# Five edits to a metaformer and mixture-of-experts kernel: where the time step's rows are spread, how the C rows, the gate and the depthwise taps are issued, and which engine adds the last image's softmax sums

## The chip, the cores and the metric

The kernel runs on one core of a Trainium2 chip. The metric is the device time of one launch in microseconds (us), as the median of several runs. Engines are named as in the profile: PE is TensorE, DVE is VectorE, ACT is ScalarE, POOL is GpSimd, and SP is SyncE, whose queue issues most DMA transfers.

## The reference, cut to what matters

The input is four images of 256 channels by 32 x 32 positions (N = 1024 positions, all in fp32). For each image the reference computes, in this order:

```python
xc = layernorm(x).reshape(B, N, 4, 64)          # four groups n of 64 channels
# for each group a Mamba block: 128 inner channels d, 16 states s
u, z = split(xc_n @ inw_n.T); u = silu(conv4(u))
dt = softplus((u @ xpw_n.T)[:, :4] @ dtw_n.T + dtb_n); Bm, Cm = the next 16 and 16 columns
h[d, s] = exp(dt * A[d, s]) * h[d, s] + dt * u * Bm[s]      # scan over the 1024 positions
y = sum_s h[d, s] * Cm[s] + u * D
xm_n = (y * silu(z)) @ outw_n.T + skip * xc_n
# convolutions, with 3-tap depthwise ones
g = sigmoid(conv1x1(depthwise3_grouped(xm)));  xg = g * xm
R = conv1x1(depthwise3(xg)) + xg
xm2 = conv1x1(depthwise3(concat[xs, R])) + xs
# beside each other: a depthwise convolution, and attention with 8 heads of 32
x_out = gelu(layernorm(concat[depthwise3(xm2), mha(xm2)] @ fc))
x_out = proj(layernorm(depthwise3x3(instance_norm(x_out))))
# then, for all 4096 positions: layer norm, a router (8 experts, top 2), two-layer experts with gelu
```

## The kernel before, in words

**Order of the work.** All engines run in the order in which Python emits instructions (a manual schedule), so the program's order is the queue of each engine. Two things make that order. The scan loop emits one *step* after the other; generators (the other stages) are advanced by `beat()`, which is called once behind each step, a *tick*. A generator that yields k is resumed k ticks later.

**The scan.** There are 32 *parts* (b, n, h): image b, channel group n (`NB` = 4), half h of the positions (512 each). A part has 16 steps i = 4q + g: g picks 32 of the 128 inner channels, q four of the 16 states, so one step is 128 rows (32 channels x 4 states) by 512 positions. In a step, `decay` (L653, ACT) makes dA = exp(dt A) three steps ahead, `inflow` (L663, DVE) makes dBu into a PSUM bank one step ahead, `step` runs the DVE scan instruction (L674) and then a POOL product with the spread C rows (L682). `spread_b` (L645) and `sums_of` (L687, L692) are PE matmuls, once per q. All PSUM tiles come from one pool of eight banks, all 128 x 512 temporaries from a pool of 16 (`act2`).

**What is emitted at which step for the next part.** The dictionaries `before`, `behind` and `group` say it. For the next part: `project_dt` at step 0, `softplus` at 2, `sum_dt` at 4 and `times_u` at 5 (both POOL), and `spread_dt` at 10, 11, 13 and 14: four DMAs each on SP's queue, copying 32 rows of dt and dt u to each of the four state groups. `spread_c` (four DMAs per q) is emitted at steps 0, 4, 8 and 13. In the second half of a group, `project_c` and `copy_c` for the next group stand at steps 3 and 5 (its first half) and 7 and 9 (its second half): a matmul of 16 rows into a bank, an ACT copy of 16 x 512, and a DMA to DRAM. For the part just finished, `project_out` stands at step 6 and `add_skip` at 8.

**Beside the scan.** When the scan of image b begins, the generator `convolutions(b - 1)` starts. It runs beside the parts (b,0,0), (b,0,1), (b,1,0) and (b,1,1), which are 64 ticks. Behind the last step of (b,1,1) a `drain()` advances the generators until the convolutions are done; then `attention(b - 1)` runs, with the scan stopped until its last blocks. The last image's convolutions and attention come behind the whole scan. There, expert tiles (`tiles`, L1994 and L2004) fill PE between the convolutions' pieces; for the attention they are held back.

**The convolutions.** In order: load (4 ticks); `depthwise3` on the input `xl`, per channel half c: the first tap on ACT (L424), then two taps on DVE (L429); the grouped convolution `qd` on PE; `gate`/`sigmoid` (L860, L870): two banks for each c, then two sigmoids that read PSUM, with a load of the sigmoid table in front and of the log/exp table behind; the product with `xm` on POOL (L878); `depthwise3` on `xm`; four products `rp` with their residual copies on ACT (L889); `depthwise3` on the result (`d4r`); four products `fp`, two ticks apart (L918); four products `vp`; eight products `qkp` (L998).

`in_turn` is what makes pipelines of a product and its use:

```python
        def in_turn(items, make, use, lag=2, every=1):
            made, lag = [], lag // every
            for at in range(len(items) + lag):
                if at >= lag:
                    use(items[at - lag], made[at - lag])
                if at < len(items):
                    made.append(make(items[at]))
                yield every
```

**Attention.** A block is (g, h): four heads and half of the queries; there are four blocks per image, each of `NK` = 8 steps kt over keys. A step: four logit matmuls `st` (L1023), four ACT exponentials `e` (L1033), four matmuls with the values (`av`, L1069). Of each pair of steps the exponentials are added on DVE (L1079, four adds), and four matmuls with ones (L1043) add the pair's sums into a second bank. At a block's end: Ln and Exp on ACT (L1051, L1056), a maximum (L1055) and a product (L1059) on DVE. The generator `local` puts six depthwise taps (L440, L445) on DVE beside the attention.

Of the kernel before, what the change touches and what calls it, by code (L numbers as in the profile page):

```python
# [9 lines left out]
F32 = mybir.dt.float32  # L10
# [62 lines left out]
def network(  # L73
# [70 lines left out]
    with tc.tile_pool(name="w_conv", bufs=1) as wp, tc.tile_pool(  # L144
# [277 lines left out]
        def depthwise3(dst, c, src, c_src, w, wi, bias):  # L422

            nc.scalar.activation(  # L424
                dst[:, c, :], src[:, c_src, 0:N], AF.Identity, bias=bias, scale=col(w, 3 * wi)
            )
            yield 1
            for k in (1, 2):
                nc.vector.scalar_tensor_tensor(  # L429
                    dst[:, c, :], src[:, c_src, k : k + N], col(w, 3 * wi + k), dst[:, c, :],  # L430
                    ALU.mult, ALU.add,
                )
                yield 1

# [188 lines left out]
        def project_c(b, n, h):  # L623
            cp = T[b, n, h, "cp"] = ps(f"cp_{b}_{n}_{h}")
            nc.tensor.matmul(
                cp[0:DS], xpwT_s[:, n, DTR + DS :], T[b, n, "u"][:, half(h)], start=True, stop=True
            )

        def copy_c(b, n, h):
            c_rows = a2(f"c_{b}_{n}_{h}", DS)  # L630
            nc.scalar.copy(c_rows, T[b, n, h, "cp"][0:DS])
            cd = T[b, n, h, "cd"] = spread.tile([DS, HALF], F32, tag="cd", name=f"cd_{b}_{n}_{h}")
            nc.sync.dma_start(cd, c_rows)
# [77 lines left out]
        def add_skip(b, n, h):  # L711
# [7 lines left out]
            1: [(sums_of, GS - 1)], 3: [(gather,)], 6: [(project_out,)], 8: [(add_skip,)],  # L719
# [4 lines left out]
            10: [(spread_dt, 0)], 11: [(spread_dt, 1)],  # L724
# [8 lines left out]
            {3: [(project_c, 0)], 5: [(copy_c, 0)], 7: [(project_c, 1)], 9: [(copy_c, 1)]},  # L733
# [3 lines left out]
        def first_part():  # L737
# [18 lines left out]
            for h in range(2):  # L756
                project_c(0, 0, h)
                copy_c(0, 0, h)
# [68 lines left out]
        def convolutions(b):  # L827
# [6 lines left out]
            for c in range(NC2):  # L834
                yield from depthwise3(d[0], c, xl, c, "fdw_w", c, col("fdw_b", c))
# [19 lines left out]
            def gate(c):  # L855
                gp = []
                for h in range(2):
                    gp.append(ps(f"gp_{b}_{c}_{h}"))
                    r = ts(h, 64)
                    nc.tensor.matmul(  # L860
                        gp[h], qpwT_s[r, ts(c, P)], qs[r], start=True, stop=True
                    )
                return gp

            gs = []

            def sigmoid(c, gp):
                gs.append(a4(f"g_{b}_{c}"))
                for h in range(2):
                    nc.scalar.activation(  # L870
                        gs[c][:, half(h)], gp[h], AF.Sigmoid, bias=col("qpw_b", c)
                    )
                loaded[0] = None
                log_exp()

            yield from in_turn(range(NC2), gate, sigmoid)
# [5 lines left out]
            for c in range(NC2):  # L882
                yield from depthwise3(d[1], c, xm, c, "rdw_w", c, col("rdw_b", c))
# [23 lines left out]
            for c in range(NC2):  # L907
                for ticks in depthwise3(
                    d[1], c, xm, c, "fdw_w", NC2 + c, col("fdw_b", NC2 + c)
                ):  # L910
                    next(gated, None)
                    yield ticks
# [91 lines left out]
        def attention(b):  # L1004
# [30 lines left out]

            log_exp()
            ahead = logits(*steps[0])
            pairs, accs, ending = [], [None, None], []

            def sum_pair():  # L1040
                kt, acc, es = pairs.pop()
# [19 lines left out]
            for at, (g, h, kt) in enumerate(steps):  # L1061
# [11 lines left out]
                if pairs:  # L1073
                    sum_pair()
# [1078 lines left out]
```

## Time and profile before

| | us |
|---|---|
| median of 3 runs (2289.41 to 2292.67) | 2289.62 |
| the profiled execution's own time | 2288.33 |
| its span in the trace | 2286.6 |
| PE busy | 2030.7 |
| DVE busy | 1556.7 |
| ACT busy | 1222.6 |
| POOL busy | 1066.4 |
| mean granted clock of PE | 0.937 of full |

Busy times are sums over the whole span. The stages have different limits, so the prediction reads the span stretch by stretch. Times of a stretch are counted from the span's start. In rows of groups, the columns are: line, engine, operation, output<-input tiles, shapes, count | busy us, mean ns of one | idle us just before them and what ended it. In a row of a table of stretches each engine has its busy us and, in brackets, its instructions.

### The profile page before, as it was taken

To read this page: it belongs to the slowest core of one execution; us is meant where nothing else is said; L and a number is where in the kernel's file an instruction comes from. 1 tells how busy PE (TensorE), PEld (TensorE's weight loads), DVE (VectorE), ACT (ScalarE), POOL (GpSimd) and SP (SyncE) were. 2 spreads that over 40 slices of the span, in tenths; PEclk is the share of its full clock that TensorE was granted. 3 is DMA by queue.
4 is the path that set the end of the run, shared out by engine and by line. 5 is a ranking of instruction groups with operands and counts; after the bars stand their busy time and mean duration, and the time that the engine had idled before them with its cause. 6 is when DMAs were issued, how large, how long until landed. Compare 5 with 4: busy or idle time off the path is not lost. (4 is left out here: it accounts for less than half of the span.)

```text
span 2286.6 us, 28565 instructions
## 1 busy us (share of the span) xinstructions
PE 2030.7 (89%) x8858; PEld 908.8 (40%) x8858; DVE 1556.7 (68%) x2217; ACT 1222.6 (53%) x2297; POOL 1066.4 (47%) x929
## 2 busy tenths in 40 slices
PE   6878878999977999986799999679999999999995
PEld 2112112332212322322123223125743768888884
DVE  3989998767899878799887877986254353211111
ACT  4665666677767666664666767334267422222221
POOL 0788878613688630675985035554040123322221
PEclk8887999999998999996899999679999999999997
DMA  3554453301453321333433013343230266877765
GB/s 98 139 155 123 125 135 89 99 10 51 98 139 86 92 48 38 93 89 95 133 89 99 19 34 78 84 157 110 87 108 1 63 198 202 243 195 195 195 175 159
DMA packets 160846, 252.86 MB, mean 111 GB/s; under 512 B 35300, under 2 KB 105348, under 8 KB 160680
## 3 DMA queue, kind: packets, MB, share of 16 engines
q1 hardware_dynamic: 140800, 225.46, 35.6%
q0 software_dynamic: 13264, 17.85, 4.1%
q10 hardware_dynamic: 6616, 7.58, 1.0%
q8 instruction: 74, 1.21, 0.2%
q14 instruction: 92, 0.75, 0.1%
HBM read 141.31 MB, written 33.98 MB: 77 GB/s over the span
## 5 line engine op out<-in xcount | busy, mean ns | idle before, releaser
L682 POOL TENSOR_TENSOR dA<-hs,cs 128x512 f32<-128x512 f32 x512 | 683.2, 1341 | 459.1 <-DVE hs L674 303.2
L653 ACT ACTIVATE dA<-dts,A 128x512 f32<-128x512 f32 x512 | 358.9, 717 | 169.7 <-DMA dts<-dt 82.2
L692 PE MATMUL yp<-dA,quads 128*32 128x512 f32 x1024 | 297.6, 667 | 86.3 <-POOL dA L682 61.8
L2020 POOL DMA_INDIRECT Y<-ys,dest x70 | 114.5, 1635 | 524.8 <-DVE ys L2014 518.5
L1033 ACT ACTIVATE e<-st 128x512 f32<-128x512 f32 x512 | 263.9, 603 | 97.4 <-PE st L1023 90.3
L663 DVE TENSOR_TENSOR dBu<-dts,bs 128x512 f32<-128x512 f32 x384 | 261.0, 680 | 76.2 <-PE bs L645 24.5
L1999 ACT ACTIVATE hs<-h,b 128x256 f32<-128x256 f32 x280 | 116.6, 472 | 354.5 <-PE h L1994 206.5
L2004 PE MATMUL y<-w,hs 128*128 128x256 f32 x1120 | 256.0, 380 | 2.8 <-ACT hs L1999 2.8
L1994 PE MATMUL h<-xT,w 128*128 128x256 f32 x1120 | 251.8, 381 | 5.1 <-DVE xT L1972 5.1
L674 DVE TENSOR_TENSOR_SCAN hs<-dA,last,dBu 128x512 f32<-128x512 f32 x192 | 244.2, 1272 | 5.0 <-ACT sq_lgn L1115 1.3
L674 DVE TENSOR_TENSOR_SCAN hs<-dA,dBu 128x512 f32<-128x512 f32 x192 | 232.3, 1210 | 9.9 <-issue 4.4
L1994 PEld LDWEIGHTS h<-xT,w 128*128 128x128 f32 x1120 | 212.9, 191 | 42.4 <-issue 7.8
L1079 DVE TENSOR_TENSOR e<-e,e 128x512 f32<-128x512 f32 x256 | 169.1, 723 | 86.2 <-ACT e L1033 51.8
L1972 DVE COPY xT<-xp 128x512 f32<-128x512 f32 x35 | 24.2, 691 | 295.7 <-PE xp L1971 295.7
L2004 PEld LDWEIGHTS y<-w,hs 128*128 128x128 f32 x1120 | 209.6, 190 | 38.4 <-issue 8.7
L645 PE MATMUL bs<-u,xpwT_s 128*32 128x512 f32 x1024 | 170.2, 678 | 53.1 <-DVE hs L674 27.4
L1023 PE MATMUL st<-qk 32*128 32x512 f32 x1024 | 173.0, 638 | 1.6 <-DVE hs L674 1.6
L692 PEld LDWEIGHTS yp<-dA,quads 128*32 128x32 f32 x1024 | 51.6, 115 | 307.2 <-POOL dA L682 177.9
L1069 PE MATMUL av<-e,v 128*32 128x512 f32 x1024 | 139.5, 604 | 0.0
L1023 PEld LDWEIGHTS st<-qk 32*128 32x128 f32 x1024 | 59.3, 183 | 115.3 <-issue 86.2
L1043 PE MATMUL av<-e,every 128*32 128x512 f32 x512 | 86.7, 594 | 4.1 <-DVE e L1079 4.1
L663 DVE TENSOR_TENSOR bs<-dts,bs 128x512 f32<-128x512 f32 x128 | 86.6, 676 | 2.2 <-DMA dts<-dt 2.2
(295 smaller groups left out, 2725.3 us busy)
## 6 DMA issues: line engine op xcount, KB each, us to landing
w<-in_W_dram SPq DMA_DIRECT2D x136, 512.0 KB, 4.5
dts<-dt SPq DMA_DIRECT2D x512, 128.0 KB, 2.3
cs<-cd SPq DMA_DIRECT2D x512, 64.0 KB, 2.1
xs<-XS SPq DMA_DIRECT2D x35, 260.0 KB, 4.5
xd<-xn SPq DMA_DIRECT2D x64, 128.0 KB, 2.5
b<-in_b_dram SPq DMA_DIRECT2D x35, 128.0 KB, 4.8
xn<-in_x_dram SPq DMA_DIRECT2D x8, 512.0 KB
XL<-xl SPq DMA_DIRECT2D x8, 512.0 KB, 2.7
```

The costliest lines, as they stand in the source:

```text
L645: nc.tensor.matmul(bs[r], xpwT_s[:, n, s : s + 1].to_broadcast([P, 32]), T[b, n, "u"][:, half(h)], start=True, stop=True,)
L653: nc.scalar.activation(dA, T[b, n, h, "dts", g][:, 0, :], AF.Exp, scale=A[:, g, n, q : q + 1])
L663: nc.vector.tensor_tensor(dBu, T[b, n, h, "dts", g][:, 1, :], T[b, n, h, "bs", q], ALU.mult)
L674: nc.vector.tensor_tensor_scan(hs, T[b, n, h, "dA", i], dBu, 0.0 if h == 0 else last, ALU.mult, ALU.add)
L682: nc.gpsimd.tensor_tensor(dA, hs, T[b, n, h, "cs", q], ALU.mult)
L692: nc.tensor.matmul(T[b, n, h, "yp"][ts(g, 32)], quads, T[b, n, h, "dA", q * GD + g], start=False, stop=(q == GS - 1),)
L1023: nc.tensor.matmul(sts[i], k[r, ts(kt, P)], q[r, half(h)], start=True, stop=not shifted)
L1033: nc.scalar.activation(es[i], sts[i], AF.Exp, scale=1.0 / HD**0.5)
L1069: nc.tensor.matmul(accs[0][ts(i, HD)], v8[:, kt, ts(4 * g + i, HD)], es[i], start=(kt == 0), stop=(kt == NK - 1),)
L1079: nc.vector.tensor_tensor(first[i], first[i], es[i], ALU.add)
L1994: nc.tensor.matmul(hp[:, i, :], w1(c, k), xT[:, c, :], start=(c == 0), stop=(c == NC2 - 1))
L2004: nc.tensor.matmul(yp[:, ts(t, C)], hs[:, k, ts(t, P)], w2(k), start=(k == 0), stop=(k == NHC - 1))
```

## The change

1. `spread_dt` for g = 0 and 1 stands at steps 7 and 9 instead of 10 and 11. `project_out` stands at step 7 (6 before), `add_skip` at 9 (8 before).
2. `project_c` makes both halves at step 3, as 32 rows each (B and C rows) in one bank; `copy_c` at step 6 copies 64 rows once, and two DMAs store the two halves' 16 C rows.
3. `depthwise3` takes both channel halves: the two first taps on ACT, one tick apart, then one more tick, then the four DVE taps.
4. The gate makes one bank per tick; ACT copies each with its bias (Identity), and behind the four copies two sigmoids of 1024 columns run from SBUF.
5. Attention: `total`, the bank of the sums, is taken with the first sum; a block's Ln and Exp stand directly behind the last sum, and its two DVE instructions in front of the next step's adds. For the last image the group of steps whose exponentials are added on DVE is all eight (`group = NK`), and the matmuls with ones run once per block.

```diff
-        def depthwise3(dst, c, src, c_src, w, wi, bias):
...
+        def depthwise3(dst, src, w, wi, bias):
+            for c in range(NC2):
+                nc.scalar.activation(
+                    dst[:, c, :], src[:, c, 0:N], AF.Identity, bias=col(bias, wi + c),
+                    scale=col(w, 3 * (wi + c)),
+                )
+                yield 1
+            yield 1
+            for c in range(NC2):
+                for k in (1, 2):
+                    nc.vector.scalar_tensor_tensor(
+                        dst[:, c, :], src[:, c, k : k + N], col(w, 3 * (wi + c) + k), dst[:, c, :],
+                        ALU.mult, ALU.add,
+                    )
+                    yield 1
...
+        def project_c(b, n):
+            cp = T[b, n, "cp"] = ps(f"cp_{b}_{n}")
+            for h in range(2):
+                nc.tensor.matmul(
+                    cp[ts(h, 2 * DS)], xpwT_s[:, n, DTR:], T[b, n, "u"][:, half(h)],
+                    start=True, stop=True,
+                )
+        def copy_c(b, n):
+            c_rows = a2(f"c_{b}_{n}", 4 * DS)
+            nc.scalar.copy(c_rows, T[b, n, "cp"][0 : 4 * DS])
+            for h in range(2):
...
+                nc.sync.dma_start(cd, c_rows[ds(2 * DS * h + DS, DS), :])
...
-            1: [(sums_of, GS - 1)], 3: [(gather,)], 6: [(project_out,)], 8: [(add_skip,)],
+            1: [(sums_of, GS - 1)], 3: [(gather,)], 7: [(project_out,)], 9: [(add_skip,)],
...
-            10: [(spread_dt, 0)], 11: [(spread_dt, 1)],
+            7: [(spread_dt, 0)], 9: [(spread_dt, 1)],
...
-            {3: [(project_c, 0)], 5: [(copy_c, 0)], 7: [(project_c, 1)], 9: [(copy_c, 1)]},
+            {3: [(project_c,)], 6: [(copy_c,)]},
...
+            yield from in_turn(
+                CO_H, gate, lambda at, gp: nc.scalar.activation(
+                    gs[at[0]][:, half(at[1])], gp, AF.Identity, bias=col("qpw_b", at[0])
+                ),
+            )
+            for c in range(NC2):
+                nc.scalar.activation(gs[c], gs[c], AF.Sigmoid)
+            loaded[0] = None
+            log_exp()
+            yield 1
...
+            group = NK if b == B - 1 else 2
+            ready, total, ending = [], None, None
+            def invert(g, h, values, total):
+                low = a2(f"low_{b}_{g}_{h}")
+                nc.scalar.activation(low, total, AF.Ln, bias=added)
...
+            def end_block(g, h, values, total, low):
+                at = (2 * b + g) * 2 + h
+                if not shifted:
+                    nc.vector.tensor_reduce(sums[:, 0, at : at + 1], total, AX.X, ALU.max)
+                nc.vector.tensor_tensor(OT[b][g][:, half(h)], values, low, ALU.mult)
+            def sum_group():
...
+                return invert(g, h, values, total) if kt == NK - 1 else None
...
+                if ending:
+                    end_block(*ending)
+                ending = sum_group() if ready else None
+                if kt % group == 0:
                     first = es
                 else:
                     for i in range(4):
                         nc.vector.tensor_tensor(first[i], first[i], es[i], ALU.add)
-                    pairs.append((kt, accs[1], first))
-                    if ending:
-                        end_block(*ending.pop())
-                if kt == NK - 1:
-                    ending.append((g, h, *accs))
+                if kt % group == group - 1:
+                    ready.append((g, h, kt, values, first))
```

## The prediction

> **What bounds the kernel now.** I read the page first, then a table of stretches, then groups and the timeline inside the stretches that the edits touch.
>
> ```profile
> span 2286.6 us, 28565 instructions
> PE 2030.7 (89%) x8858; PEld 908.8 (40%) x8858; DVE 1556.7 (68%) x2217; ACT 1222.6 (53%) x2297; POOL 1066.4 (47%) x929
> ```
>
> PE's 89% is an average. Parts of the scan with nothing beside them last 27.3 to 28.3 us (16 scan starts 1.7 to 1.8 apart) and DVE never waits there; the rest is mixed. The table takes image 2: parts (2,0,0), (2,0,1), (2,1,0), (2,1,1) up to the first logit matmul, the attention beside the stopped scan, and last the attention of the last image.
>
> ```profile
> core 0: us, PE busy (x) PEld busy (x) DVE busy (x) ACT busy (x) POOL busy (x), PEclk, DMA share, GB/s
> 676.60:711.20 34.60, 25.50 (x103) 6.50 (x102) 33.30 (x37) 26.52 (x49) 27.96 (x22) 0.95 0.54 139
> 711.20:751.60 40.40, 32.23 (x116) 8.63 (x114) 36.80 (x39) 28.14 (x41) 33.74 (x24) 0.87 0.36 89
> 751.60:791.20 39.60, 38.33 (x124) 14.33 (x125) 30.52 (x36) 21.68 (x45) 25.64 (x20) 1.00 0.36 89
> 791.20:821.80 30.60, 30.40 (x121) 11.28 (x119) 27.84 (x31) 21.00 (x38) 23.44 (x20) 1.00 0.39 92
> 821.80:918.70 96.90, 95.91 (x638) 26.51 (x634) 77.36 (x106) 70.39 (x140) 6.07 (x5) 1.00 0.09 24
> 1677.80:1764.20 86.40, 86.40 (x642) 24.52 (x641) 51.41 (x79) 69.52 (x137) 19.96 (x27) 1.00 0.13 39
> ```
>
> In the first two rows DVE is the bound and PE idles 9.1 and 8.2 us; from the third row to the end of the attention PE has almost no gap (1.3, 0.2, 1.0). In the last row PE is busy all the time. From 1600 us to 2235 PE idles only some 10 us in all, so the tail is PE work laid end to end.
>
> What DVE waits for in part (2,0,1), and in part (2,1,0):
>
> ```profile
> L429 DVE SCALAR_TENSOR_TENSOR d<-xm,V,d 128x1024 f32<-128x1024 f32 x4 | 6.1, 1528 | 3.6 <-ACT d L424 3.6
> ```
>
> ```profile
> L663 DVE TENSOR_TENSOR dBu<-dts,bs 128x512 f32<-128x512 f32 x13 | 8.9, 683 | 7.2 <-ACT u L582 3.2 <-ACT xm L715 3.1 <-PE bs L645 0.6
> ```
>
> The 3.6 is ACT being late with the first tap. The 7.2 is different: ACT itself waits there for PE (6.5 us for `up`, 5.0 for `op`), whose queue is full of `fp` products.
>
> Last image's attention, from the timeline: two steps, and the end of the last block.
>
> ```profile
> 1691.61 2.50 DVE L1079 TENSOR_TENSOR e<-e,e 128x512 f32<-128x512 f32 x4 [0.43 <-PE av L1069]
> 1692.31 1.14 PE L1023 MATMUL st<-qk 32*128 32x512 f32 x8
> 1693.38 1.07 PE L1069 MATMUL av<-e,v 128*32 128x512 f32 x8
> 1693.47 4.13 ACT L1033 ACTIVATE e<-st 128x512 f32<-128x512 f32 x8 [1.07 <-PE st L1023]
> 1694.03 2.48 DVE L445 SCALAR_TENSOR_TENSOR xloc<-xl,V,xloc 128x1024 f32<-128x1024 f32 x2
> 1696.54 1.04 PE L1043 MATMUL av<-e,every 128*32 128x512 f32 x8
> 1697.51 0.71 PE L1023 MATMUL st<-qk 32*128 32x512 f32 x4
> ```
>
> ```profile
> 1760.67 2.50 DVE L1079 TENSOR_TENSOR e<-e,e 128x512 f32<-128x512 f32 x4 [2.70 <-ACT e L1033]
> 1762.13 2.14 PE L1043 MATMUL av<-e,every 128*32 128x512 f32 x8
> 1764.30 0.69 ACT L1051 ACTIVATE low<-av,added 128x512 f32<-128x512 f32 x1 [2.83 <-PE av L1043]
> 1765.02 0.69 DVE L1055 TENSOR_REDUCE sums<-av 128x1 f32<-128x512 f32 x1 [1.86 <-ACT low L1051]
> 1765.78 0.69 DVE L1059 TENSOR_TENSOR qk<-av,low 128x512 f32<-128x512 f32 x1
> ```
>
> A pair of steps takes 5.20 us (1692.31 to 1697.51), all PE. ACT needs 4.13 of them, DVE 2.50 for four adds.
>
> **The change, part by part.**
>
> *Last image's sums.* Per block, four sets of `ones` matmuls (1.0 us each) become one: 12 us of PE go, in four blocks. Adds go from 4 to 7 sets of 2.50. Then PE needs 8 x 2.07 + 1.0 = 17.6 us per block, ACT 8 x 2.07 + 1.5 = 18.0, DVE 17.5 for adds. But a block's end is now serial: the last add ends at 1763.17, the product at 1766.47, so 3.3 us pass through PE, Ln and the maximum, and the next block's adds stand behind the product. DVE's period is 17.5 + 3.3 = 20.8 us against 21.3 now (second logit sets of successive blocks start at 1704.85, 1726.14, 1747.43). The six `local` taps (1.6 + 2.5 + 2.5 us), which lie in DVE's idle time now, are no longer hidden. First adds 3.75 us behind the first logits, as now; 4 x 17.5 + 3 x 3.3 + 6.6 = 86.5 more; last add at 90.2 us where it is at 85.4: **+4.8**. Bounds: -2 (taps hidden, four blocks 0.5 shorter each) to +9 (PE, now 85% busy, falls to half clock for some 3 us per block, as it does in the stretches of 0.95 and 0.87 above). PE work saved gives nothing, because the tiles are held until the attention is over. The Trainium skill, "PSUM — Partial Sum Buffer", PSUM bank collisions raise a hardware error, has two engines on one bank kept apart by semaphores; the row that shows DVE's maximum waiting for ACT's Ln agrees, and it speaks against this edit.
>
> *Length of the convolutions.* Counting yields: before, 4 + 6 + 3 + 1 + 4 + 2 + 6 + 4 + 6 + 12 + 6 + 10 = 64 ticks (load, taps, `qd`, its copy, gate, product, taps, `rp`, taps, `fp`, `vp`, `qkp`), exactly the four parts. After: each `depthwise3` has 7, the gate 7, so 70. Everything behind the gate comes 4 to 6 ticks later, and six ticks fall into the drain.
>
> *(b,0,0).* First taps in front and single gate banks remove DVE's waits for ACT's `d` and `g`: 2.5 us for image 1, 1.2 for image 2, 6.0 for image 3: **-9.7** in all.
>
> *(b,0,1).* The 3.6 goes (DVE's first tap is three ticks behind ACT's, not one) and two of the `d4r` taps (1.25 each) move on: -6.1. Against it, the sigmoids now come in a lump at step 4: loads 2 x 1.28 and 2 x 1.05 (row of the equally wide `z` silu), 4.7 us, behind softplus (2.7), four copies (2.8), y (0.6) and five decays (3.6): 14.4 us of ACT in steps that last 8.9; decays run three steps (5.3 us) ahead. Bounds 0 and 3.7 of new DVE wait; I take 1.5, near the lower end because ACT is ahead otherwise. POOL's `xm` products now follow dt in its queue and end before DVE's taps. **-4.6** x 3 = -13.8. Loads go from four to two per image, 2.6 us of ACT; copies cost 2.7 and sigmoids 2.1 where four took 2.7: nothing. By the Trainium skill, "ScalarE: Activation LUTs", What ACT_TABLE_LOAD costs, a switch also pays a drain of about 1.38 us, which would save another 2.8; here a sigmoid starts 0.02 us behind its 1.28 load, so I leave that out.
>
> *(b,1,0) and (b,1,1).* In the new program's order the last two `rp` products fall behind the boundary: half of 7.5 + 4.2 us, +5.9 of PE. The `fp` products stand behind steps 9, 11, 13, 15 instead of 3, 5, 7, 9. Until step 9 DVE then sets the pace: 9 x 1.71 + 4 x 1.25 = 20.4 us. PE has there what it has now up to 769.5 less two `fp` products (16.6 - 9.9), plus 5.9, about 14 with the leftovers: 6.4 us idle, 5.1 more than the 1.3 now. From there PE is full until the first logits (in the drain three `qkp` products). Cost 5.9 + 5.1 = 11; if PE starts `fp` one step early (its sums are ready then), 9. I take **+9** x 3 = 27. Bounds: 0 (all of it hides in DVE's time) and 14 (the drain's six ticks at DVE-step length, 10.5, instead of 5.2).
>
> *dt rows earlier.* ACT waits 82.2 us for them in 29 waits, but DVE does not wait for ACT there: pure parts run at 27.3 with these waits in them. What moves: eight DMAs per part pass in front of `spread_c` at step 8, on SP's queue. SP's longest wait for dt u is 5.2 us, and those C rows are used at step 12, four steps (6.8 us) on. **0**, bounds -3 and +3.
>
> *C rows in one bank.* 16 ACT copies of 0.57 us go (9.1), two DMAs come together at step 6; matmuls stay. ACT is not the bound where they stand: 0, bounds -3 and 0. `project_out` and `add_skip` one step later: their wait (3.1) is PE's queue, so 0.
>
> *Attention of images 0 to 2* keeps pairs, PE stays full, Ln comes one step earlier: 0 +- 2. *Last image's convolutions* are six ticks longer, but tiles fill PE meanwhile and the attention still starts behind the fifth tile: 0, bounds -2 and +3.
>
> Sum: 4.8 - 9.7 - 13.8 + 27 = +8.3 on the profiled execution's 2288.3, 2296.6; the median of the runs is 1.3 higher. I say **2297**.
>
> **Rivals.**
>
> *Faster (0.25).* The shifted products hide: PE work is the same in total, and if the spread of `fp` over (b,1,0) and (b,1,1) leaves no new gap, the +27 is near 0 and the waits removed are gained. For it: DVE has 8.1 us of waits in (2,1,0) that a different order could dissolve. Against: PE has no gap left there to hide 5.9 us in. 4.8 - 9.7 - 13.8 = -18.7: 2271. It decides for faster as soon as the +9 is under +2 per image.
>
> *No change (0.15).* The +9 is about 5 to 7, or the attention's +4.8 is 0: 2285 to 2294.
>
> *Much slower (0.08).* The drain is exposed in full (14 instead of 9 per image: +15) and the last attention pays 9: 2288.3 + 8.3 + 15 + 4.2 = 2316.
>
> *My forecast (0.52)*: 2294 to 2312.
>
> **How the numbers follow.** 0.2%, about what a measurement of this kernel can tell from no change, is 4.6 us. Faster has the first rival's 0.25 less its edge, 0.24; same 0.16; slower 0.60. The range leaves out the lower half of the first rival and most of the third: 2277 to 2314. The likeliest case's own range is 2294 to 2312.
>
> **What would show it.** In the profile after: no wait of L429 for ACT in (b,0,1), and that part near 36 us; PE gaps of 4 us or more in the first half of (b,1,0); image 2's way from its first scan step to its first logits 2 to 4 us longer than 145.2; four blocks of the last attention 20 to 21 us apart, DVE busy nearly throughout, PE with gaps at each block's end, and the whole near 91 us. I am wrong if PE is without gaps in (b,1,0), if the drain costs nothing, or if the last attention gets shorter than 86.

## The result, and the profile after

The changed kernel takes 2330.89 us (median of 4 runs, 2327.64 to 2333.63), the kernel before 2290.35 beside it (4 runs): 1.0175 times as long, interval 1.0157 to 1.0193. The forecast was 2297, with a range up to 2314. The profiled execution took 2327.64 us with a span of 2325.5; it is compared with the 2288.33 and 2286.6 of before, so 38.9 us of span have to be found.

The head of the page, after:

```profile
span 2325.5 us, 28564 instructions
PE 2047.4 (88%) x8830; PEld 922.4 (40%) x8830; DVE 1582.3 (68%) x2273; ACT 1224.4 (53%) x2291; POOL 1072.1 (46%) x932
```

PE is busy for 16.7 us more, although 96 of its 512 products with ones went (86.7 us in all before, 79.2 after). Most of the reason is at the end of the timeline of PE (start, length, engine, line, tiles, count, idle time before), first before, then after:

```profile
2240.03 7.07 PE L2004 MATMUL y<-w,hs 128*128 128x256 f32 x32
```

```profile
2247.74 5.13 PE L2013 MATMUL y<-w,hs 128*128 128x256 f32 x23
2252.80 0.19 PE L1485 MATMUL any<-most,ones_mean 128*1 128x1 f32 x2
2269.78 1.08 PE L1980 MATMUL xp<-ident,xs 128*128 128x128 f32 x4 [16.79 <-SPq L1920]
2271.64 8.68 PE L2003 MATMUL h<-xT,w 128*128 128x256 f32 x32 [0.78 <-DVE xT L1981]
2280.16 7.07 PE L2013 MATMUL y<-w,hs 128*128 128x256 f32 x32
```

The first row after ends the 35th expert tile, with which the kernel before ended (there at 2247.1 us, here at 2252.9). Then PE waits 16.79 us, and a 36th tile follows, which did not run before: 34.4 us from the one tile's last product to the other's. The wait is long because the last four tiles of the program stand under a condition, are loaded by SP only once the condition is known, and have nothing beside them:

```python
            with tc.If(used > n - LATE):          # LATE = 4, LATEST = 3
                for i in range(n - LATE, n - LATEST):
                    whole_tile(i)
                ...                               # the last three, under a second condition
```

`used` is counted from the router's choices: per expert, its rows in tiles of 256, rounded up. So the time of this kernel depends on values. Without the 36th tile the trace would be 5.8 us longer than before up to the last product, where the steps of the prediction sum to 8.3.

The same stretches as before, by image 2's parts and both kinds of attention:

```profile
core 0: us, PE busy (x) PEld busy (x) DVE busy (x) ACT busy (x) POOL busy (x), PEclk, DMA share, GB/s
677.00:710.50 33.50, 28.40 (x100) 6.72 (x100) 33.50 (x38) 23.94 (x46) 27.87 (x22) 0.90 0.58 144
710.50:746.30 35.80, 29.01 (x91) 6.57 (x90) 34.65 (x38) 25.52 (x38) 31.97 (x24) 0.81 0.45 112
746.30:780.80 34.50, 34.32 (x122) 11.14 (x121) 33.68 (x38) 25.72 (x49) 27.90 (x20) 1.00 0.36 89
780.80:822.20 41.40, 40.77 (x149) 17.47 (x147) 27.82 (x31) 20.38 (x35) 24.53 (x20) 1.00 0.30 74
822.20:918.80 96.60, 95.57 (x635) 26.48 (x634) 77.24 (x106) 71.40 (x141) 5.13 (x4) 0.98 0.08 23
1677.00:1768.20 91.20, 86.43 (x554) 22.97 (x554) 80.30 (x129) 72.78 (x141) 30.63 (x25) 0.98 0.12 35
```

The four scan rows sum to 145.2 us, exactly as before (34.6 + 40.4 + 39.6 + 30.6). Parts (2,0,0) and (2,0,1) are 1.1 and 4.6 shorter, and the last two rows together, the way from (2,1,0) to the first logits, are 5.7 longer. In the third row PE is busy for 34.32 of 34.50 us: there is no gap in which anything could wait.

DVE's two waits that the prediction showed, in parts (2,0,1) and (2,1,0) after (the line of the taps is now L433, that of `inflow` L672):

```profile
L433 DVE SCALAR_TENSOR_TENSOR d<-xm,V,d 128x1024 f32<-128x1024 f32 x4 | 6.4, 1598 | 0.0
```

```profile
L672 DVE TENSOR_TENSOR dBu<-dts,bs 128x512 f32<-128x512 f32 x13 | 8.8, 679 | 0.7 <-ACT xl L918 0.7
```

The 3.6 us wait for the first tap is gone, and of 7.2 us in (2,1,0) 0.7 are left: the taps of `d4r` now lie there.

### The profile page after: what moved, and what is told of

It is laid out like the page before. It is cut to its first block, busy times and chain, and to the rows that moved or that the text cites. A ratio compares the mean times of both kernels' runs of the same rounds, so it can differ in the third digit from the quotient of the medians.

```text
span 2325.5 us, 28564 instructions
## 1 busy us (share of the span) xinstructions
PE 2047.4 (88%) x8830; PEld 922.4 (40%) x8830; DVE 1582.3 (68%) x2273; ACT 1224.4 (53%) x2291; POOL 1072.1 (46%) x932
## 3 DMA queue, kind: packets, MB, share of 16 engines
q1 hardware_dynamic: 142672, 227.96, 34.6%
## 5 line engine op out<-in xcount | busy, mean ns | idle before, releaser
L691 POOL TENSOR_TENSOR dA<-hs,cs 128x512 f32<-128x512 f32 x512 | 691.5, 1358 | 415.0 <-DVE hs L683 276.6
L701 PE MATMUL yp<-dA,quads 128*32 128x512 f32 x1024 | 312.1, 667 | 99.4 <-POOL dA L691 72.4
L672 DVE TENSOR_TENSOR dBu<-dts,bs 128x512 f32<-128x512 f32 x384 | 260.5, 679 | 64.0 <-PE bs L654 33.1
L2003 PE MATMUL h<-xT,w 128*128 128x256 f32 x1152 | 261.9, 383 | 4.9 <-DVE xT L1981 4.9
L2013 PE MATMUL y<-w,hs 128*128 128x256 f32 x1152 | 264.5, 381 | 1.9 <-ACT hs L2008 1.9
L1091 DVE TENSOR_TENSOR e<-e,e 128x512 f32<-128x512 f32 x304 | 195.1, 711 | 72.9 <-PE av L1080 50.0
L2003 PEld LDWEIGHTS h<-xT,w 128*128 128x128 f32 x1152 | 220.6, 192 | 47.6 <-issue 11.0
L2013 PEld LDWEIGHTS y<-w,hs 128*128 128x128 f32 x1152 | 216.9, 191 | 38.2 <-issue 7.9
L1080 PE MATMUL av<-e,v 128*32 128x512 f32 x1024 | 146.4, 611 | 0.0
L1776 POOL DMA_INDIRECT XS<-XR,to x64 | 82.0, 1281 | 15.7 <-issue 9.9
L672 DVE TENSOR_TENSOR bs<-dts,bs 128x512 f32<-128x512 f32 x128 | 86.6, 677 | 3.5 <-DMA dts<-dt 3.4
```

The source lines that it names most:

```text
L672: nc.vector.tensor_tensor(dBu, T[b, n, h, "dts", g][:, 1, :], T[b, n, h, "bs", q], ALU.mult)
L691: nc.gpsimd.tensor_tensor(dA, hs, T[b, n, h, "cs", q], ALU.mult)
L701: nc.tensor.matmul(T[b, n, h, "yp"][ts(g, 32)], quads, T[b, n, h, "dA", q * GD + g], start=False, stop=(q == GS - 1),)
L1080: nc.tensor.matmul(values[ts(i, HD)], v8[:, kt, ts(4 * g + i, HD)], es[i], start=(kt == 0), stop=(kt == NK - 1),)
L1091: nc.vector.tensor_tensor(first[i], first[i], es[i], ALU.add)
L2003: nc.tensor.matmul(hp[:, i, :], w1(c, k), xT[:, c, :], start=(c == 0), stop=(c == NC2 - 1))
```

## Why a tile more: a read that passed a write

The new `depthwise3` emits the first taps of both halves one tick apart. For `d4r` this puts the second half's first tap in front of the residual's last write into the tile that it reads. The timeline of ACT, image 0's convolutions, first before, then after:

```profile
373.71 0.69 ACT L889 ACTIVATE xm<-rp,V 128x512 f32<-128x512 f32 x1 [1.28 <-PE rp L395]
377.46 1.23 ACT L424 ACTIVATE d4r<-xm,V 128x1024 f32<-128x1024 f32 x1
```

```profile
380.89 1.24 ACT L425 ACTIVATE d4r<-xm,V 128x1024 f32<-128x1024 f32 x1
382.16 0.69 ACT L892 ACTIVATE xm<-rp,V 128x512 f32<-128x512 f32 x1
```

The write replaces xg in `xm` by R (the names of the reference). So in the changed kernel that tap takes, for channels 128 to 255, the second half of the positions as xg and not as R; the two DVE taps come later and read R. Program order decides what is read, and the dependencies follow it, so nothing waits. The theory: these slightly different values move rows between experts, and a rounded-up count goes up by one. The rivals: the other rounding of the new arithmetic does it (sums added on DVE, bias apart from the sigmoid), or a late tile is only a matter of time.

**Changed kernel, the write back in front of the read.**

```diff
+            next(gated, None)
             for ticks in depthwise3(d[1], xm, "fdw_w", NC2, "fdw_b"):
-                next(gated, None)
                 yield ticks
+                next(gated, None)
```

> The changed kernel with one thing undone, and no tick added or taken: the residual's last write of xm (use (1,1)) stands again in front of d4r's first tap of the second half of the channels, as it does in the kernel before. Theory, values: that tap read xm before its residual was added, so the router's counts moved and a 36th expert tile ran. Then this kernel runs 35 tiles (1120 h products, not 1152), the 34.3 us between the 35th tile's last product and the 36th's go, and 5 to 6 us are left over the kernel before: 2295 to 2297. Rival, rounding: the new order of the arithmetic (sums added on VectorE, bias and sigmoid apart) tips a count; then 1152 products stay, and 2328 to 2333. Rival, time alone: a tile is late and not additional; then 1152 stay as well.

Measured: 2296.75 us against 2293.99 (1.001, 0.9998 to 1.0022), and 35 tiles in the groups of its profile:

```profile
L2004 PE MATMUL h<-xT,w 128*128 128x256 f32 x1120 | 253.4, 382 | 4.1 <-DVE xT L1982 4.1
```

**The kernel before, with that one read moved.**

```diff
-            for c in range(NC2):
-                for ticks in depthwise3(d[1], c, xm, c, "fdw_w", NC2 + c, col("fdw_b", NC2 + c)):
-                    next(gated, None)
-                    yield ticks
+            taps = [depthwise3(d[1], c, xm, c, "fdw_w", NC2 + c, col("fdw_b", NC2 + c)) for c in range(NC2)]
+            for c, early in ((0, False), (0, True), (0, False), (None, False), (1, False), (1, False)):
+                if early:
+                    next(taps[1])
+                if c is not None:
+                    next(taps[c])
+                next(gated, None)
+                yield 1
```

> The kernel before with that one read moved and nothing else: d4r's first tap of the second half of the channels is issued two ticks earlier, in front of the residual's last write of xm, so it takes that half's second 512 columns without the residual (this changes the computation there). Theory, values: 1152 h products, a gap of some 17 us on PE in front of the last 32, and 33 to 35 us over the kernel before: 2323 to 2326. Rivals, rounding or time: 1120 products, and 2288 to 2292.

Measured: 2328.53 against 2293.99 us (1.0148, 1.0129 to 1.0167), 34.5 more in the medians. Its groups show 144 transposes `xp` (4 per tile, so 36 tiles) and the wait in front of the last four:

```profile
L1976 PE MATMUL xp<-ident,xs 128*128 128x128 f32 x144 | 22.1, 277 | 16.3 <-SPq L1916 16.3
L1999 PE MATMUL h<-xT,w 128*128 128x256 f32 x1152 | 264.2, 386 | 6.5 <-DVE xT L1977 6.5
```

Both directions hold. The moved read is necessary and enough; rounding and time alone are out, since the first kernel has all the new arithmetic and its timing, and the second has none of it. Of the 40.5 us some 34 to 35 are the tile. What the change does to the schedule is +2.8 by this run (-0.5 to +5.0) and 5.8 in the trace of the changed kernel up to the 35th tile's end, with a forecast of +7 to +8.

## The rest of the sum, edit by edit

The runs of this section were taken on several chips, each beside the kernel before, whose median lies between 2289.6 and 2294.0 us; so the differences are to be compared, not the times.

**The attention's edit alone**, on the kernel before: the last image's `group = NK`, Ln and Exp behind the last sum, `end_block` in front of the adds, as in the change's diff.

> The kernel before with the edit of the attention alone (last image's sums added on VectorE, Ln one step earlier). The trace after shows 3.0 us more from the last image's first logits to its output product where the prediction said 4.8, and 1 less over the other three images: so 2292 to 2294, 35 tiles. If the prediction's term was right and images 0 to 2 give nothing: 2295. Rival, the DVE time hides beside the tiles and the PE work saved counts: 2288 or less. Rival, rounding: 1152 h products and 2325 or more.

Measured: 2295.24 against 2293.99 us (1.0003, 0.9985 to 1.0021), 35 tiles. The median does not tell +3 from nothing. Its profile has 92.6 us from the last image's first logits to its output product, where the kernel before had 88.3: +4.3, near the 4.8. But here the granted clock is 0.72 in two slices of 6 us, from 1702 and from 1714 us. In the four other kernels with this edit the way takes 91.1 or 91.2 us, +2.8 or +2.9, and in one of them (64 ticks, below) the clock is 1.00 over the whole of it. So the term was over-sized by some 2 us, and the 1.5 us more of this profile stand beside its two slow slices; the prediction's upper bound had such a loss in it. The changed kernel at the end of the last block, the wait of PE and two slices of 6 us:

```profile
1762.79 3.60 PE L1066 MATMUL sum<-e,every 128*32 128x512 f32 x8 [2.21 <-DVE e L1091]
```

```profile
1756.00:1762.00 6.00, 4.58 (x28) 1.22 (x24) 6.00 (x11) 3.48 (x7) 0.00 (x0) 1.00 0.00 0
1762.00:1768.00 6.00, 5.21 (x16) 2.23 (x17) 3.33 (x7) 1.52 (x4) 0.00 (x0) 0.72 0.00 0
```

PE waits there 2.21 us for DVE's last adds, and the granted clock is 0.72 in the six microseconds that hold the end of that gap; before it was 1.00 in both. The kernel with 64 ticks has the same gap of 2.21 us and keeps its clock:

```profile
1757.00:1763.00 6.00, 3.79 (x13) 1.40 (x13) 4.14 (x8) 0.79 (x2) 0.00 (x0) 1.00 0.00 0
```

**The scan's own edits alone** (dt rows at steps 7 and 9, C rows in one bank, two steps shifted, on the kernel before).

> The kernel before with the scan's own edits alone: dt rows sent at steps 7 and 9, C rows of both halves in one bank, project_out and add_skip one step later. The prediction gave them nothing. The trace after shows one place where VectorE newly waits, 1.1 us in part (0,0,1) for the POOL product of dt, and 7.0 us in (3,0,0) for the same product. Theory, only the first is theirs, since the second stands where other waits were taken away: 0 to +2 over the kernel before. Rival, both are theirs: +6 to +8, with a wait of 4 us or more of the scan for dt in (3,0,0). Rival, the earlier dt rows free ScalarE: 3 us or more faster.

Measured: 2288.91 against 2289.57 (0.9993, 0.9982 to 1.0005). Nothing in the median, as forecast, and the wait of the scan for dt in (3,0,0) is 1.6 us, as before. The 7.0 in the changed kernel is not theirs: it is there with the convolutions' edits alone, which come next. The trace shows more than the median: the way from (b,1,0) to the first logits is 69.0 us in each of the three images, 1.1 or 1.2 shorter than before, and the three parts (b,0,0) are together 4.7 longer. Two other kernels with the old convolutions in that part have 1.7 and 2.6 more there, so how much of the 4.7 belongs to these edits is open.

**The convolutions' edits alone** (gate, first taps in front, with the write in its place).

> The kernel before with the convolutions' edits alone (gate bank by bank with the two sigmoids together, first taps of both halves in front), the residual's last write kept in front of d4r's second first tap. 35 expert tiles. Theory: all three movements of the scan seen after are theirs, -6.3 in (b,0,0), -13.0 in (b,0,1), +17.6 behind them, and the last image's convolutions last 2.7 longer: together +1, and so -1 to +3 against the kernel before. The prediction's steps: -9.7 - 13.8 + 27 and 0, +3.5. Rival, part of the gain in (b,0,1) came from the dt rows sent earlier: (b,0,1) stays at 38 or more and the sum is +6 or more.

Measured: 2303.11 against 2289.57 (1.0055, 1.0037 to 1.0074), 13.5 us slower. The theory and the prediction's steps missed; the rival's +6 or more was met, but not its sign, since (b,0,1) lasts 37.7, 36.5 and 36.5 us. The three groups of edits alone, -0.7, +13.5 and +1.3, sum to 14.1, where all together with the read put back are at +2.8. That is more than the intervals make likely, so the groups seem to belong together. What differs is in DVE's waits of part (2,0,1) and in the C products' group; here with the convolutions' edits alone:

```profile
L667 DVE TENSOR_TENSOR dBu<-dts,bs 128x512 f32<-128x512 f32 x13 | 8.8, 680 | 2.2 <-ACT c L635 1.6 <-ACT g L868 0.6
```

```profile
L629 PE MATMUL cp<-u,xpwT_s 128*16 128x512 f32 x64 | 33.2, 601 | 0.2 <-ACT u L748 0.2
```

The scan's `inflow` waits for a bank that ACT's copy of C rows still holds; in the program's order the sigmoids stand in front of that copy. Two further kernels add one half of the scan's edits each to this one.

```diff
-            {3: [(project_c, 0)], 5: [(copy_c, 0)], 7: [(project_c, 1)], 9: [(copy_c, 1)]},
+            {3: [(project_c,)], 6: [(copy_c,)]},
```

> The kernel with the convolutions' edits alone (13.5 us over the kernel before) with one more of the change's edits: the C rows of both halves in one bank. dt rows stay at steps 10 and 11. Open is what makes that kernel some 11 us slower than the whole change with its read put back, where the scan's own edits alone give nothing. Theory, C rows: the two C products of a group now stand in different columns and run side by side (64 of them keep PE busy for 18.2 us after, 33.9 before), which counts where the convolutions' edits fill PE, and VectorE's wait of 1.6 for ScalarE's C copy in (b,0,1) goes. Then 2291 to 2296, and first logits 76 us behind the start of (b,1,0) instead of 78.3. Rival, the dt rows sent earlier: nothing changes, 2300 to 2305. Rival, half from each: 2297 or so.

```diff
-            10: [(spread_dt, 0)], 11: [(spread_dt, 1)],
+            7: [(spread_dt, 0)], 9: [(spread_dt, 1)],
```

> The counterpart: the convolutions' edits with dt rows sent at steps 7 and 9, project_out and add_skip one step later, C rows as in the kernel before. Theory, C rows: 2300 to 2304, the wait of 1.6 for the C copy in (b,0,1) stays, first logits 78 behind (b,1,0). Rival, dt rows: 2291 to 2296 and no such wait. Rival, half from each: 2297.

Measured: with the C rows 2293.38 against 2293.08 (0.9999, 0.9984 to 1.0014), with the dt rows 2301.48 against the same (1.0041, 1.0024 to 1.0058). So of the +13.5 the C rows take about 13. The dt rows take about 5, which the intervals (8.5 to 16.9 without them, 5.5 to 13.3 with them) do not tell from nothing, and their kernel keeps the wait of 1.6 us for the copy. The C products in the first of the two:

```profile
L630 PE MATMUL cp<-u,xpwT_s 128*32 128x512 f32 x64 | 18.0, 606 | 0.0
```

Each of the 64 still lasts 0.6 us, but together they keep PE busy for 18.0 instead of 33.2: two of them, 32 columns wide each and side by side in one bank, run at the same time. Where PE has no gap this is time: from (b,1,0) to the first logits the three images take 76.6 or 76.7 us with it and 78.3 to 78.5 without (77.2 with the dt rows), and `inflow` no longer waits for the copy (0.6 left, all of it for g), which makes (b,0,1) another 0.6 to 0.7 shorter. From (b,0,0) to the first logits the three images take together 455.6 us with the convolutions' edits alone, 448.2 with the C rows and 455.1 with the dt rows (447.7 before). These are 7.4 of the 14.3 us between the first two traces; the rest is spread over other stretches, by less than 2 us each, and is not explained.

**Six ticks less, in two ways.** First without the empty ticks and with the gate's banks two by two:

```diff
                 yield 1
-            yield 1
             for c in range(NC2):
                 for k in (1, 2):
...
-            yield from in_turn(CO_H, gate, ...)
+            yield from in_turn(range(NC2), gate, copy_gate)   # two banks, two copies each
...
             log_exp()
-            yield 1
```

> The first kernel of this list with the convolutions cut back from 70 ticks to 64: no empty tick behind the first taps (3), and the gate's banks copied two by two without a tick behind the sigmoids (3). Everything else of the change stays. Theory: the 5.9 us per image in (b,1,0) and (b,1,1), 17.6 in all, come from the six ticks alone, and the 19 us gained in (b,0,0) and (b,0,1) come from the order of the taps: 2295.5 less 17 or so is 2278 (2275 to 2283). Rival: the gain of 13 in (b,0,1) is only work that left that part for the next, so both go back together: 2290 to 2294. Rival: VectorE again waits for ACT's first taps, which are two ticks ahead instead of three: 2283 to 2288.

Then, with all 70 ticks' order up to that point, by setting the `fp` products on successive steps:

```diff
-                ), mixed, lag=2 if b == B - 1 else 4, every=1 if b == B - 1 else 2,
+                ), mixed,
```

> The first kernel of the list before (changed kernel, the residual's write back in its place) with one more edit: the four fp products of images 0 to 2 stand on successive steps instead of every other one, so the convolutions of these images take six ticks fewer (64) with the same work. Theory, PE full: in the trace after PE idles 0.8 of the 75.9 us from (b,1,0) to the first logits, so their length is PE's work and not the number of ticks: -2 to +2 against that kernel, 2295 to 2299, first logits 75 to 76 us behind the start of (b,1,0). The prediction's reason, ticks and idle PE: the 70.1 us of the kernel before come back, 17.6 us less: 2279. Rival, the products come before their sums are ready and hold up the queue: 3 us or more longer.

Measured: 2287.16 against 2293.99 (0.9974, 0.9963 to 0.9986) and 2291.99 against 2289.57 (1.0014, 1.0004 to 1.0025). In the first one, part (2,0,1) goes back to 40.3 us and the way from (2,1,0) to the first logits to 70.2, together 110.5; the kernel before has 110.6 (40.4 + 70.2), the changed one 111.7 (35.8 + 75.9), the one with its read put back 112.5 (35.8 + 76.7), the dense one 111.2 (36.5 + 74.7). Wherever the border lies, the sum stays within 2 us. So the first rival of the 64 ticks, work that only changes its part, had the mechanism right for images 0 to 2, though not the time. The second rival has 2287 in its range, but its wait did not come: in (2,0,1) DVE's taps wait for nothing (0.0). What the 64 ticks gain is mostly the last image's: 158.4 us from the scan's end to its first logits, against 161.1 before, 163.8 after and 164.4 with the read put back. The dense kernel is 2.4 over its own kernel before, the one that it stands on was 2.8 over its own: no difference, as its theory said. The dense products show the limit from the other side; the row of their stretch from (2,1,0) to the first logits:

```profile
744.80:819.50 74.70, 73.84 (x272) 28.30 (x270) 61.59 (x67) 46.51 (x84) 51.47 (x39) 1.00 0.33 82
```

Six ticks less, and PE still idles only 0.9 us: 76.7 becomes 74.7, not 70.1. The length is PE's work.

**64 ticks, and the last image's sums in pairs again** (`group = 2`).

> The kernel with 64 ticks of the list before (2287.2, 6.8 under the kernel before) with the last image's sums in pairs again, as images 0 to 2 have them. Theory: the way from the last image's first logits to its output product goes back from 91.1 to 88.2 us, and PE keeps full clock there (after, it falls to 0.72 for the 6 us that follow a gap of 2.2): 2283 to 2285, 9 to 11 us under the kernel before. The prediction's term says 4.8 less: 2282. Rival, the PE work of 12 us more is paid beside the tiles: 2287 or more.

Measured: 2284.25 against 2289.57 (0.9974, 0.9958 to 0.999), 5.3 less. The last attention is back at 88.7 us with PE busy throughout. The 9 to 11 us expected did not come: against its own kernel before, the kernel with 64 ticks alone gained 6.8, so a gain by the pairs, if there is one, is inside the intervals.

**Work moved out of the full stretch.** Three fifths of each `fp` product depend only on early values.

```diff
+            early = in_turn(CO_H, lambda at: product(f"fp0_...", fpwT_s, at[0],
+                [d[0][:, ci, half(at[1])] for ci in range(NC2)], xl[...]),
+                lambda at, r: nc.scalar.copy(xl[...], r)) if beside else iter(())
             for c in range(NC2):
                 nc.gpsimd.tensor_tensor(xm...)
+                next(early, None)
                 yield 1
-            yield from depthwise3(d[1], xm, "rdw_w", 0, "rdw_b")
+            for ticks in depthwise3(d[1], xm, "rdw_w", 0, "rdw_b", beside):
+                next(early, None)
+                yield ticks
...
-                    [d[ci // 2][:, ci % 2, half(at[1])] for ci in range(4)],
+                    [d[ci // 2][:, ci % 2, half(at[1])] for ci in range(NC2 if beside else 0, 4)],
```

> A try at a faster kernel, from what the runs show: PE has no gap from (b,1,0) to the first logits of images 0 to 2, and 6 to 8 us of idle time at less than full clock in (b,0,1). Of the fp products three fifths (xl and the first two chunks) depend on nothing that is computed late; they go beside the rdw taps in (b,0,1), ScalarE copies their sums into xl, and the late product adds the other two chunks to it (one more pass of xl through PE, 4.3 us per image, and four more copies of 0.7). It stands on the kernel with dense fp products (2.4 over the kernel before), with the last image's sums in pairs and without the empty ticks in the last image's convolutions. Theory: 7.5 us of PE less where PE is full, 5 to 7.5 of it per image gained (15 to 22), 3 to 4 by the pairs, 2 to 3 by the last image's ticks: 2261 to 2272. Rival, part (b,0,1) grows by as much, because PE runs there at half clock and VectorE waits for banks: 2284 to 2290. Rival, VectorE sets the end of (b,1,1) as soon as PE is let off: 2274 to 2280.

Measured: 2290.49 against 2293.08 (0.9986, 0.9971 to 1.0); its runs spread from 2282.02 to 2295.07, and the profiled one is near the low end (2282.94). The first logits of the three images come 67.8 us behind (b,1,0), 7 less than 74.7, as PE's work says. But (2,0,1) grew to 40.7:

```profile
L673 DVE TENSOR_TENSOR dBu<-dts,bs 128x512 f32<-128x512 f32 x13 | 8.9, 683 | 7.2 <-ACT xl L888 3.3 <-ACT c L638 2.2 <-ACT g L873 1.5
```

The early copies stand behind ACT's first taps, which wait for POOL, and hold banks. The rival of a longer (b,0,1) took about half of the gain, and in the profile 6.5 us more were lost behind the last image's output product (491.2 us to the last expert tile's end, 484.7 in the dense kernel).

> The kernel with the fp products in two halves, mended in the two places where its profile gave the time back. First, the early halves begin two ticks behind d's first tap instead of beside POOL's xm products: in the profile their copies stand on ScalarE's queue behind the first taps, which wait for POOL, hold banks, and VectorE waits 3.3 us for them in (b,0,1), which lasts 40 us instead of 36. Second, the last image's convolutions take 64 ticks again (gate banks two by two there): with 70 or 66 the way from the last image's output product to its last variance is 102.3 to 102.5 us long in five profiles, with 64 it is 98.6. Theory: 2 to 4 us per image in (b,0,1) and 4 to 10 behind the attention: 2272 to 2280, 13 to 20 under the kernel before of the same chip. Rival, the wait moves to d4r's taps and PE's gain is lost there: 2284 to 2288. Rival, PE's work in the tail sets the end whatever comes before: 2288 to 2292, as the one before.

```diff
+            # the last image's gate: in_turn(range(NC2), ...), two banks, two copies each
...
             for c in range(NC2):
                 nc.gpsimd.tensor_tensor(xm...)
-                next(early, None)
                 yield 1
-            for ticks in depthwise3(d[1], xm, "rdw_w", 0, "rdw_b", beside):
-                next(early, None)
+            for at, ticks in enumerate(depthwise3(d[1], xm, "rdw_w", 0, "rdw_b", beside)):
+                if at:
+                    next(early, None)
                 yield ticks
```

Measured: 2275.24 against 2293.5 us (0.9916, 0.9897 to 0.9935), 18.3 less than the kernel before and the fastest of all kernels run here. The stretches of image 2 (parts and drain, as in the tables above):

```profile
706.90:744.60 37.70, 31.21 (x110) 9.50 (x109) 35.32 (x38) 26.61 (x41) 31.93 (x24) 0.95 0.45 112
744.60:783.40 38.80, 37.95 (x133) 13.38 (x133) 33.91 (x38) 28.98 (x56) 27.65 (x20) 1.00 0.33 82
783.40:814.80 31.40, 31.40 (x126) 12.84 (x124) 27.75 (x31) 18.86 (x30) 23.67 (x20) 1.00 0.38 94
```

In this profile (b,0,1) is 3 us shorter than in the one before, but the way from (b,1,0) to the logits is 2.4 to 4.1 longer (70.2 for image 2), so the three images together are no faster (434.9 against 434.1 us). The theory was wrong there. The first rival had it right that PE's gain shrinks, but not why: the taps of `d4r` wait for nothing in image 2, and PE itself is busy for 69.35 us of the way instead of 66.94, since 16 of the 24 `rp` matmuls of image 2, not 12, now fall into it. The three images are 12.8 us faster than in the kernel before (447.7). Behind the attention the theory held: 98.6 us from the last image's output product to its last variance, where the kernel with 66 ticks had 102.3. The expectation's count was wrong, though: of seven profiles with 66 or 70 ticks four have 102.3 to 102.5 and three 99.4 to 101.1; all seven with 64 have 98.6. The medians of the two kernels are 15.2 apart and their profiled executions 3.6 (2282.94 and 2279.35): the one is 7.5 under its median, the other 4.1 over its own. Why the first one's runs spread over 13 us is open; no profile shows its slower ones.

## Why the prediction was wrong, and where it was right

The step that failed is one that was not in the sum at all: it took the tail as a fixed amount of "PE work laid end to end" and costed the first taps' edit as order alone. It compared the queues for who waits for whom, not for which value a moved read finds. No rival held it either; that the change does something else than it says was a rival to name. In its place the runs showed a 36th expert tile of 34.4 us: it is gone with that one read put back (+2.8 in all), and it comes with that one read moved (+34.5).

| step | forecast | profile after | what the runs add |
|---|---|---|---|
| expert tiles | 35, unsaid | 36: +34.4 | the moved read, both ways |
| last image's sums | +4.8 | +2.8 (88.3 to 91.1) | +4.3 alone, where the clock falls twice |
| (b,0,0), three images | -9.7 | -6.3 | |
| (b,0,1), three images | -13.8 | -13.0 | |
| (b,1,0) to first logits | +27 | +17.4 | PE's work, not ticks |
| dt rows | 0 | | about -5 with the convolutions' edits, not told from 0 |
| C rows | 0 | | about -13 with the convolutions' edits |
| dt and C rows without the convolutions' edits | 0 | | 0 in the median |
| attention of images 0 to 2 | 0 | -1.1 | |
| last image's convolutions | 0 | +2.7 (161.1 to 163.8) | 158.4 with 64 ticks |
| last output product to the 35th tile's end | 0, unsaid | +3.6 (481.1 to 484.7) | 480.4 to 491.2 over all kernels; tied to no edit |

*(b,0,0)* is short by 3.4 because in image 3 a new wait took the place of those removed. DVE's waits for `g` (3.2) and `d` (2.8) go, and the scan now waits for the POOL sum of dt, whose inputs hold the buffer that the scan is to write:

```profile
L683 DVE TENSOR_TENSOR_SCAN hs<-dA,dBu 128x512 f32<-128x512 f32 x12 | 14.5, 1209 | 8.2 <-POOL dt L612 7.0 <-POOL apart L1775 1.2
```

POOL sends rows to the experts there, one indirect DMA between any two of its products for the scan, and its sum of dt comes 17.3 us behind the part's start, 18.8 before: 1.5 us earlier, not 6.0.

*(b,0,1)* was right to 0.8, and with it the reading of the wait for `d`.

*(b,1,0)* was over-sized by one of its two terms. The 5.9 us of `rp` work that falls behind the border came, as 5.4 (12 of the 24 `rp` matmuls of image 2), and the way is 5.8 longer per image. The 5.1 of idle PE until step 9 did not come: PE idles 0.2 us in the third row. The prediction said that it would be wrong if PE had no gaps there, and it had none; the 64 ticks and the dense products show the same.

*C rows.* "Matmuls stay" was true of their number and false of their time (33.9 us of PE before, 18.2 after), and "ACT is not the bound where they stand" was true only of the kernel before. With the sigmoids in a lump in (b,0,1), ACT's copy is what `inflow` waits for. Two edits were priced one by one against the trace of before, and the runs suggest that one of them changed what the other is worth.

*Last image.* The six ticks do cost there, 2.7 us, at the upper end of the bounds (+3). Over all kernels the way takes 159.4 to 161.1 us with the old convolutions and 162.8 to 164.4 with 70 ticks, so the cost may be somewhat larger. "Tiles fill PE meanwhile" did not make it nothing. The last image's sums were over-sized: 2.8 was measured for 4.8.

Without the tile the medians would be at +2.8 where +7 to +8 was said, inside the range and within 0.2% of no change. That the rest of the sum, 8.3, lies near the 5.8 of the trace is partly luck: the 9.6 too much in (b,1,0), 2.0 in the last image's sums and 1.1 in the other attentions are balanced by 3.4, 0.8, 2.7 and 3.6 too little elsewhere. Two slips change nothing: DVE's waits in (2,1,0) before are 9.1 us (7.2 and 1.9), not 8.1, and the sum with its 1.3 gives 2297.9, not 2297.

## What to carry to other kernels

When instructions are moved, follow the tiles as well as the queues: a read that passes a write of the same tile needs no wait, so no profile shows it but the order of the rows. Where trip counts or conditions depend on computed values, count the instructions of the stages that the change does not touch before explaining any time. Price edits that meet in one stretch together: a copy or a product that cost nothing counts as soon as another edit takes the slack in front of it.

## What the runs showed of the hardware

- Two matmuls with 32 columns each, side by side in one bank, overlap: 64 of 0.6 us keep PE busy for 18.0 us; with 16 columns, four steps apart and each at the start of a bank of its own, for 33.2. The kernel before already had this in its `bs` products, four of them side by side in a bank (L645: 1024 of 0.68 us in 170.2 us). The Trainium skill, "TensorEngine Tiling (Array Packing)", Key Properties, says the same of tiles of the array: they operate independently and can run their matmuls in parallel.
- A gap of 2.21 us on PE was followed by a granted clock of 0.72 over 6 us at the end of the last attention; a gap of 2.46 us in the same kernel (at 1699.7 us) was followed by 1.00, and so was one of 3.13 us in the kernel before (at 1832.1 us). By the Trainium skill, "TensorE: Matmul & The Clock Gate", Why this matters for your kernels, it takes gaps of more than about 3 us. The runs agree only in part: a shorter gap was followed by a lower clock, a longer one was not. Nor does the length alone decide: the gap of 2.21 us at the end of the last attention stands in five kernels, and the clock of the next 6 us is 0.72 in three of them (changed, read put back, dense) and 1.00 in two (attention alone, 64 ticks). What decides it is not shown here.
- A tile that is loaded only when its condition is known costs 34.4 us, of which 16.8 are PE waiting for rows and weights; a tile in the packed tail costs 14.2.
